# Feed-forward with tokens on the free axis: a feature-major first feed-forward in a two-layer gated cross-attention kernel

## The chip, the cores and the metric

The kernel runs on one core of a Trainium2 chip. A core has a matrix engine (TensorE, PE in the profile; PEld is its loading of the stationary operand), a vector engine (VectorE, DVE), an engine for activation functions (ScalarE, ACT), a general one (GpSimd, POOL) and SyncE (SP), which issues most of the transfers. Each runs its own queue of instructions in order, and semaphores tie the queues together. SBUF is the on-chip memory of 128 partitions; TensorE writes its products to PSUM, 128 partitions in eight banks of 512 fp32 columns. The metric is the device time of one execution in microseconds.

## The reference

Four batches of 512 tokens with 512 features go through two layers, each of a gated cross-attention and a gated feed-forward. The change touches the first layer's feed-forward, and in one place the weights of the second's.

```python
def act_quant(x):                      # per token
    scale = 127.0 / jnp.clip(jnp.max(jnp.abs(x), axis=-1, keepdims=True), EPS)
    q = jnp.clip(jnp.round(x * scale), -128.0, 127.0) / scale
    return q
def weight_quant(w):                   # ternary
    scale = jnp.clip(jnp.mean(jnp.abs(w)), EPS)
    return jnp.clip(jnp.round(w / scale), -1.0, 1.0) * scale
def h_bitlinear(x, w):
    return jnp.einsum('bsh,oh->bso', act_quant(fwht(x)), weight_quant(w))

gate = h_bitlinear(h, w_gate)          # 512 -> 2048
up   = h_bitlinear(h, w_up)            # 512 -> 2048
y    = h_bitlinear(silu(gate) * up, w_down)    # 2048 -> 512
...
x = x + tanh(g_xattn[0]) * L0_xattn(ctx, layernorm(x))   # similarity of 512 x 512, top 153 a row
x = x + tanh(g_ffn[0])   * L0_ffn(layernorm(x))          # the above
x = x + tanh(g_xattn[1]) * L1_xattn(layernorm(x), ctx)   # 16 heads, rotary, softmax
x = x + tanh(g_ffn[1])   * L1_ffn(layernorm(x))          # gated, ternary weights, no Hadamard transform
```

`fwht` is the normalized Walsh-Hadamard transform along the features. The transform of `silu(gate) * up` has length 2048 = 16 x 128. The 8-bit rounding takes a scale from each token's greatest magnitude over all 2048 transformed features.

## The kernel before

**Outer order.** Attention of the second layer (`attention`, L877, class `Pair`) runs over 4 batches times 8 pairs of heads, each in four steps (`scores` L815, `turn` L840, `attended` L848, `added` L861). Everything else is background work written as generators that yield a cost. The loop at L989 advances the attention by one step and then as many parts of the background as the summed costs allow: `before(b)` (L963) for batch b = 1 to 3 during the attention of batch b - 1, that is top-k adjacency (`adjacency`, L410), keys and the first feed-forward (`feed0`, L500); then `last_weights` (L974) and the second feed-forward (`feed1`, L575) of batches 0 to 2 during the attention of batch 3. Batch 0's first feed-forward comes before the attention and batch 3's second feed-forward after it; there the flag `alone[0]` is true, and `feed0` notes it as `quick`. A scheduler of the tile framework orders each engine's queue from the program's order, given priorities and its own cost figures; the top-k instructions get a lowered priority (L446, L451), a few attention products a raised one.

**Buffers.** Background work that is not alone takes its PSUM tiles from two banks (`psb`, tag `bg`): `bg_ps` (L72), `gate_ps` (L75) and `bg_tr` (L78) all come to that. Attention has four banks (`ps`) and two more for its transposes (`pst`). SBUF tiles of 2 KB a partition have pools of two or three (`front_t` L86, `gate_t` L91, `back_t` L96), 8 KB tiles (`big` L101) a pool of three.

**First feed-forward, one tile of 128 tokens.** `zq` holds the quantized, transformed input as [feature, token], four blocks of 128 features in bf16. The weights `wa` are fp8 ternary values, [feature, 2 x 2048], those of `up` first.

- `gated` (L295), four rounds `o` of 512 hidden features: `pg` and `pu`, each [token, 512], from four accumulating products with `zq` as the stationary operand and 512 columns of `wa` moving. ScalarE computes `sg = silu(dg * pg)` straight from PSUM, with `dg` the token's scale per partition (L307), VectorE multiplies by `pu` into `ya` (L308).
- `back` in `feed0` (L545): four butterfly stages on VectorE (eight halves of 1024 columns, L551) make the transform across the 16 blocks of 128. For the transform within blocks, four times: four fp32 transposes (L557), a ScalarE copy (`yT`, L559), four fp32 products of 128 columns with the 128 x 128 Hadamard matrix moving (L563), and a scaled copy to `yb` (L564).
- `projected` (L362): maximum of magnitudes along the 2048 columns (L377), a scale per token (`scales`, L187), multiplication and addition of 12582912, which rounds (L382), subtraction to bf16 (`unmagic`, L205; L210 when not alone), 16 bf16 transposes back to [feature, token] with four ScalarE copies (`turned`, L197), and 16 products of 512 columns with the last weights `wd` (L399). L569 scales and adds to the residual.

`tiles` (L313) weaves the gates of one tile with the back part of the one before it.

**Last weights.** `ternary` (L215) reads each weight matrix in pieces of 1 MB: one pass for the mean magnitude (L234), one for the scaling and addition of 12582912 (L247) and the sign to fp8 (L248), all on ScalarE. With `hold` (first layer) the pieces stay in SBUF between the passes; without (`w1`, twelve pieces) they are read again.

Of the kernel before, what the change touches and what calls it, by code (L numbers as in the profile page):

```python
# [2 lines left out]

# [12 lines left out]
P = 128  # L16
# [10 lines left out]
EPS = 1e-5  # L27
MAGIC = 12582912.0
GONE = -3.0e38
F8 = mybir.dt.float8e4  # L30


@with_exitstack
def flamingo_kernel(
# [43 lines left out]
    def bg_tr(name, dt=F32):  # L78
        if mine("tr", 4):
            return psb.tile([P, 4, P], dt, tag="bg", name=name)  # L80
        return pst.tile([P, 4, P], dt, tag="tr", name=name)
# [14 lines left out]
    def back_t(name):  # L96
        return two_k("back", 2, name)
# [117 lines left out]
    def ternary(specs, names, hold):  # L215


        found = []

        def piece(src, inner, i, name):  # L220
            t = big(f"{name}{i}")
            marks["load"] = nc.sync.dma_start(
                t if inner == 1 else t.rearrange("p (c o) -> p c o", c=inner), src(i)
            )
            return t

        for (src, inner, n, dst, count), name in zip(specs, names):
            acc = small.tile([P, n], F32, tag=f"wacc{n}", name=f"acc_{name}")
            held = []
            for i in range(n):  # L230
                t = piece(src, inner, i, f"sa_{name}")
                held.append(t)
                junk = bp.tile([P, FF], BF, tag="q", name=f"ja_{name}{i}") if hold else t
                nc.scalar.activation(junk, t, AF.Abs, accum_out=acc[:, i : i + 1])  # L234
                yield 4.0
            tot = small.tile([P, 1], F32, tag="wtot", name=f"tot_{name}")
            nc.vector.tensor_reduce(tot, acc, AX.X, ALU.add)
            pt = bg_ps(f"pt_{name}")
            marks["sum"] = nc.tensor.matmul(pt[:, 0:1], ones, tot, start=True, stop=True)
            sc = const.tile([P, 1], F32, tag=f"ws_{name}", name=f"ws_{name}")  # L240
            nc.vector.tensor_scalar(sc, pt[:, 0:1], 1.0 / count, EPS, ALU.mult, ALU.max)
            inv = const.tile([P, 1], F32, tag=f"wi_{name}", name=f"wi_{name}")
            nc.vector.reciprocal(inv, sc)
            found.append(sc)
            for i in range(n):
                t = held[i] if hold else piece(src, inner, i, f"sb_{name}")
                nc.scalar.activation(t, t, AF.Identity, scale=inv, bias=magic[:, 0:1])  # L247
                marks["sign"] = nc.scalar.activation(  # L248
                    dst(i), t, AF.Sign, bias=magic[:, 1:2], saturate=False
                )  # L250
                yield 4.0
        return found
# [42 lines left out]
    def gated(u, zq, wa, dg, y):  # L295

        for o in range(4):
            pg = gate_ps(f"pg_{u}_{o}")
            pu = gate_ps(f"pu_{u}_{o}")
            for pw, at in ((pg, FF + o * 512), (pu, o * 512)):  # L300
                for c in range(NC):
                    nc.tensor.matmul(  # L302
                        pw, zq[:, c, :], wa[:, c, at : at + 512],
                        start=(c == 0), stop=(c == NC - 1),
                    )
            sg = gate_t(f"sg_{u}_{o}")
            nc.scalar.activation(sg, pg, AF.Silu, scale=dg)  # L307
            nc.vector.tensor_tensor(y[:, o * 512 : (o + 1) * 512], sg, pu, ALU.mult)  # L308
            yield 0.9

    reached = []

    def tiles(name, ready, wa, back, spread):  # L313

        def gate(j):
            zq, dg, du = ready[j]
            y = big(f"ya_{name}_{j}")  # L320
            return gated(f"{name}_{j}", zq, wa, dg, y), back(j, y, du)

        def go(gen, parts):
            for _ in range(parts):
                next(gen, None)

        if not alone[0]:
            last = iter(())
            for j in range(NT):
                if j == 2:  # L330
                    reached.append(name)
                front, behind = gate(j)
                yield from woven(front, last)
                last = behind
            yield from last
            return
        if spread:
            lent.extend("btbhtbbt")
        front, cur = gate(0)
        drain(front)  # L340
        last = None
        for j in range(NT):
            front, after = gate(j + 1) if j + 1 < NT else (iter(()), None)
            for k in range(8 if spread else 4):
                if spread:
                    go(cur, 1)
                if k % 2 == 0 or not spread:
                    go(front, 1)
                yield 0.0
            if spread:  # L350
                if last:
                    go(last, 4)
                go(cur, 4)
            else:
                go(cur, 4)
            if last:
                drain(last)
            last, cur = cur, after
        drain(last)
        yield 0.0  # L360

    def projected(u, z, mul, wd, gd, last):  # L362
# [35 lines left out]
        for c in range(NF):  # L398
            nc.tensor.matmul(  # L399
                pd, zT[:, c, :], wd[:, c, :], start=(c == 0), stop=(c == NF - 1)  # L400
            )
        return pd, col


# [95 lines left out]
    def feed0(b, w):  # L500
# [44 lines left out]
        def back(j, ya, du):  # L545
            u = f"f{b}_{j}"
            yb = big(f"yb_{u}")

            for src, dst, g in ((ya, yb, 8), (yb, ya, 4), (ya, yb, 2), (yb, ya, 1)):
                for args in butterfly(src, dst, "p (g t q) -> p g t q", {"g": g}):  # L550
                    nc.vector.tensor_tensor(*args)  # L551
                    yield 1.3
            for k in range(4):
                pt = bg_tr(f"ph_{u}_{k}")
                for c in range(4):
                    at = (4 * k + c) * P
                    nc.tensor.transpose(pt[:, c, :], ya[:, at : at + P], ident)  # L557
                hT_ = back_t(f"yT_{u}_{k}")
                nc.scalar.copy(hT_, pt.rearrange("p c q -> p (c q)"))  # L559
                pz = bg_ps(f"pzh_{u}_{k}")  # L560
                for c in range(4):
                    cols = slice(c * P, (c + 1) * P)
                    nc.tensor.matmul(pz[:, cols], hT_[:, cols], had_sb, start=True, stop=True)  # L563
                nc.scalar.activation(  # L564
                    yb[:, k * 512 : (k + 1) * 512], pz, AF.Copy, scale=1.0 / math.sqrt(FF)
                )
                yield 0.3
            pd, col = yield from projected(u, yb, du, wd, gd, j == NT - 1)
            nc.vector.scalar_tensor_tensor(xs[b, j], pd, col, xs[b, j], ALU.mult, ALU.add)  # L569
            yield 0.8  # L570

# [567 lines left out]
```

## Time and profile before

| | us |
|---|---|
| median of three timed runs | 2063.09 (2061.5 to 2064.79) |
| profiled execution, its own time | 2064.35 |
| its span, first to last instruction | 2062.6 |
| busy: TensorE / weight loads / VectorE | 1853.7 / 873.3 / 1584.7 |
| busy: ScalarE / GpSimd | 1176.6 / 333.1 |
| start of the attention of batches 1, 2, 3 (its transposed input, L722) | 661, 1078, 1495 |
| end of each tile of the first feed-forward (L569), batch 1 | 534, 573, 627, 651 |
| the same, batch 2 | 953, 997, 1038, 1064 |
| the same, batch 3 | 1370, 1414, 1455, 1482 |

How to read it: a row of costly groups names the line, the engine, the operation, the output and inputs by the program's names, shapes and count; then busy time in all, mean ns of one, the engine's idle time just before these instructions, and what ended that. A plain fp32 product appears as two TensorE instructions, a transpose or a bf16/fp8 product as one. Matmuls overlap in the records, so that the mean of one is longer than the spacing between two. Times are from the start of the span.

### The profile page before, as it was taken

What the parts mean: (1) busy time and instruction counts of PE and PEld (TensorE: products, weight loads), DVE (VectorE), ACT (ScalarE), POOL (GpSimd) and SP (SyncE); (2) the same over time, 40 slices, a digit from 0 to 9 for tenths busy, and PEclk for the clock granted to TensorE, in tenths of its full rate; (3) what the DMA queues carried; (4) which work ended last, traced back from release to release, by engine and by line L of the source; (5) the groups of instructions that cost most, each with busy time, mean ns of one, the idle gap of its engine ahead of it and who ended that gap; (6) DMA issues with size and microseconds to landing.
All of it is one profiled execution on the core that took longest, in us unless ns stands there. A gap on an engine that the chain in (4) does not pass through costs nothing. (4 is left out here: it accounts for less than half of the span.)

```text
span 2062.6 us, 21752 instructions
## 1 busy us (share of the span) xinstructions
PE 1853.7 (90%) x7274; PEld 873.3 (42%) x7274; DVE 1584.7 (77%) x3233; ACT 1176.6 (57%) x1979; POOL 333.1 (16%) x316
## 2 busy tenths in 40 slices
PE   1268789999999999999999999999999999999898
PEld 0035434434544444445453444454444444444344
DVE  7989599986774999876769999767636755866775
ACT  6935454455544555455454554554899565567554
POOL 3010031122100221230011221300112210101000
PEclk6579899999999999999999999999999999999999
DMA  7451021210101222110012221101755111111000
GB/s 273 148 177 38 1 77 41 63 46 27 38 21 32 83 82 60 43 38 26 27 33 87 72 73 38 38 21 33 256 191 199 50 38 45 58 35 39 11 16 26
DMA packets 65633, 139.25 MB, mean 68 GB/s; under 512 B 7537, under 2 KB 18161, under 8 KB 62449
## 3 DMA queue, kind: packets, MB, share of 16 engines
q1 hardware_dynamic: 60048, 121.92, 18.7%
q0 software_dynamic: 4320, 14.16, 1.8%
q10 hardware_dynamic: 1152, 1.77, 0.2%
q8 instruction: 58, 0.95, 0.2%
q14 instruction: 55, 0.44, 0.1%
HBM read 117.90 MB, written 19.92 MB: 67 GB/s over the span
## 5 line engine op out<-in xcount | busy, mean ns | idle before, releaser
L793 POOL TENSOR_TENSOR ro<-ro,rs 128x512 f32<-128x512 f32 x192 | 252.7, 1319 | 1167.2 <-DVE rs L789 753.8
L834 ACT ACTIVATE pp<-pss,nm 128x512 f32<-128x512 f32 x256 | 175.1, 688 | 224.8 <-DVE nm L831 224.0
L764 PE MATMUL pqh<-hT,wq 128*128 128x512 f32 x512 | 239.6, 603 | 6.8 <-ACT pp L834 6.6
L853 PE MATMUL pc<-pT,kv 128*128 128x512 f32 x512 | 235.4, 598 | 0.7 <-ACT pT L846 0.6
L865 PE MATMUL po<-om,cxo 128*128 128x512 f32 x512 | 230.9, 597 | 0.0
L831 DVE TENSOR_REDUCE nm<-pss 128x1 f32<-128x512 f32 x256 | 167.6, 681 | 57.4 <-PE pss L826 56.5
L779 PE MATMUL pb<-qh,wc 128*128 128x512 f32 x384 | 191.1, 614 | 10.4 <-ACT qh L769 7.3
L449 DVE MAX8 m<-work 128x8 f32<-128x512 f32 x304 | 198.0, 680 | 0.6
L454 DVE MATCH_REPLACE8 work<-m,work 128x512 f32<-128x512 f32 x288 | 192.8, 674 | 0.1
L837 ACT ACTIVATE pp<-pp,rsm 128x512 f32<-128x512 f32 x256 | 178.9, 724 | 21.2 <-DVE rsm L836 20.9
L870 DVE SCALAR_TENSOR_TENSOR x<-po,gt,x 128x512 f32<-128x512 f32 x128 | 94.6, 744 | 92.4 <-PE po L865 91.9
L846 ACT COPY pT<-ppt 128x512 f32<-128x512 f32 x256 | 142.9, 592 | 28.9 <-PE ppt L845 28.8
L845 PEld LDWEIGHTS ppt<-ident,pp 128*128 128x128 f32 x1024 | 117.3, 141 | 86.0 <-issue 33.9
L845 PE MATMUL ppt<-ident,pp 128*128 128x128 f32 x1024 | 146.4, 277 | 6.7 <-ACT pT L846 3.5
L823 PE MATMUL pss<-kr,qr 64*128 64x512 f32 x256 | 144.3, 644 | 5.6 <-ACT pp L834 4.8
L764 PEld LDWEIGHTS pqh<-hT,wq 128*128 128x128 f32 x512 | 92.7, 191 | 125.4 <-issue 84.6
L826 PE MATMUL pss<-kr,qr 64*128 64x512 f32 x256 | 144.4, 645 | 0.5 <-DVE ro L787 0.5
L865 PEld LDWEIGHTS po<-om,cxo 128*128 128x128 f32 x512 | 93.7, 190 | 114.5 <-issue 98.1
L787 DVE TENSOR_TENSOR ro<-pb,cos_q 128x512 f32<-128x512 f32 x192 | 130.5, 680 | 11.0 <-PE pb L779 10.2
L853 PEld LDWEIGHTS pc<-pT,kv 128*128 128x128 f32 x512 | 92.7, 190 | 102.3 <-issue 88.7
L858 ACT COPY cxo<-pc 128x512 f32<-128x512 f32 x64 | 37.6, 587 | 135.7 <-PE pc L853 135.4
L750 PE MATMUL pr<-ro,wr 128*64 128x512 f32 x192 | 99.8, 613 | 14.3 <-POOL ro L793 12.2
(266 smaller groups left out, 3123.5 us busy)
## 6 DMA issues: line engine op xcount, KB each, us to landing
wq<-in_wqh SPq DMA_DIRECT2D x64, 256.0 KB, 2.7
om<-omd SPq DMA_DIRECT2D x64, 256.0 KB, 2.7
wc<-in_wkcq SPq DMA_DIRECT2D x32, 384.0 KB, 3.1
krd<-krs POOLq DMA_DIRECT2D x32, 256.0 KB, 2.4
kr<-krd SPq DMA_DIRECT2D x32, 256.0 KB, 2.7
sa_w1v<-in_gvT SPq DMA_DIRECT2D x8, 1024.0 KB, 5.3
sb_w1v<-in_gvT SPq DMA_DIRECT2D x8, 1024.0 KB, 5.5
wr<-in_wqr SPq DMA_DIRECT2D x32, 192.0 KB, 2.4
```

What stands on the lines that cost most here:

```text
L449: nc.vector.max(m8[j], cur[j])
L454: nc.vector.match_replace(works[j], m8[j], cur[j], GONE)
L764: nc.tensor.matmul(pq, self.wqs[i][:, c, :], hT[self.b][:, c, :], start=(c == 0), stop=(c == NC - 1),)
L779: nc.tensor.matmul(pb, self.wc[:, at : at + P], self.qhs[i if i < 2 else o], start=True, stop=True)
L793: nc.gpsimd.tensor_tensor(ro, ro, rs, ALU.add)
L826: nc.tensor.matmul(*args, start=True, stop=True)
L831: nc.vector.tensor_reduce(nm, pss[i], AX.X, ALU.max, negate=True)
L834: nc.scalar.activation(pp, pss[i], AF.Exp, bias=nm, accum_out=sm)
L837: nc.scalar.activation(pp, pp, AF.Copy, scale=rs)
L845: nc.tensor.transpose(pt[:, l, :], pp[:, l * P : (l + 1) * P], ident)
L853: nc.tensor.matmul(pc, kv[self.b][:, l, :], self.pT[i][:, l, :], start=(l == 0), stop=(l == NT - 1),)
L865: nc.tensor.matmul(po, self.cxo[i][:, j * P : (j + 1) * P], self.oms[i], start=(i == 0), stop=(i == 1),)
```

## The change

For batches 1 to 3 the first feed-forward stays in [feature, token] from the gates to the last product:

- `gated_turned` takes `wa` as the stationary operand, a block of 128 hidden features at a time, and 128 tokens of `zq` as the moving one: 16 products of 128 columns into each `pg` and `pu`. The token's scale now varies along the free axis, so `dg` is spread into a 128 x 128 tile, transposed by a product with the identity, copied to SBUF as a row, and VectorE multiplies `pg` by it before ScalarE's Silu.
- In `back` the transposes and their copies are left out; the Hadamard matrix is the stationary operand and 512 columns of `ya` move, four products in all.
- `projected_turned` takes the maximum over the 16 blocks (a strided view), transposes the 128 x 128 result, takes the maximum over partitions' values, makes the scale, turns it into a row as above, multiplies all 2048 columns by the row, rounds by an addition and a subtraction in one instruction to bf16, and goes into the last product with no transposes.
- In `ternary` the scaling of pieces that are read again moves from ScalarE to VectorE.

The tile's values in `back` outside these places are as before, and batch 0 keeps the old way (`quick`).

```diff
@@ ternary
-                nc.scalar.activation(t, t, AF.Identity, scale=inv, bias=magic[:, 0:1])
+                if not hold:
+                    nc.vector.tensor_scalar(t, t, inv, MAGIC, ALU.mult, ALU.add)
+                else:
+                    nc.scalar.activation(t, t, AF.Identity, scale=inv, bias=magic[:, 0:1])
@@ new, beside gated
+    def gated_turned(u, zq, wa, dg, y):
+        row = front_t(f"dgr_{u}")
+        nc.vector.tensor_scalar(row[:, :P], ones, dg, None, ALU.mult)
+        pt = bg_ps(f"pdg_{u}")
+        nc.tensor.matmul(pt[:, :P], row[:, :P], ident, start=True, stop=True)
+        nc.scalar.copy(row[:, P : 2 * P], pt[:, :P])
+        row = row[:, P : 2 * P].unsqueeze(1).to_broadcast([P, 4, P])
+        for o in range(4):
+            pg = gate_ps(f"pg_{u}_{o}")
+            pu = gate_ps(f"pu_{u}_{o}")
+            for pw, at in ((pg, FF + o * 512), (pu, o * 512)):
+                for f in range(4):
+                    cols = slice(at + f * P, at + (f + 1) * P)
+                    for c in range(NC):
+                        nc.tensor.matmul(
+                            pw[:, f * P : (f + 1) * P], wa[:, c, cols], zq[:, c, :],
+                            start=(c == 0), stop=(c == NC - 1),
+                        )
+            sg = gate_t(f"sg_{u}_{o}")
+            nc.vector.tensor_tensor(
+                sg.rearrange("p (f t) -> p f t", f=4), pg.rearrange("p (f t) -> p f t", f=4), row, ALU.mult
+            )
+            nc.scalar.activation(sg, sg, AF.Silu)
+            nc.vector.tensor_tensor(y[:, o * 512 : (o + 1) * 512], sg, pu, ALU.mult)
+            yield 0.9
@@ gate(j), in tiles
-            return gated(f"{name}_{j}", zq, wa, dg, y), back(j, y, du)
+            made = gated_turned if spread and not alone[0] else gated
+            return made(f"{name}_{j}", zq, wa, dg, y), back(j, y, du)
@@ new, beside projected
+    def projected_turned(u, z, mul, wd, gd):
+        most = front_t(f"most_{u}")
+        nc.vector.tensor_reduce(
+            most[:, :P], z.rearrange("p (c t) -> p t c", t=P), AX.X, ALU.max, apply_absolute_value=True
+        )
+        yield 2.3
+        pt = bg_tr(f"pmx_{u}")
+        nc.tensor.transpose(pt[:, 0, :], most[:, :P], ident)
+        amax = small.tile([P, 1], F32, tag="amax", name=f"amaxh_{u}")
+        nc.vector.tensor_reduce(amax, pt[:, 0, :], AX.X, ALU.max)
+        m, sc = scales(amax, mul, f"h{u}")
+        nc.vector.tensor_scalar(most[:, P : 2 * P], ones, sc, None, ALU.mult)
+        pt = bg_tr(f"psc_{u}")
+        nc.tensor.matmul(pt[:, 0, :], most[:, P : 2 * P], ident, start=True, stop=True)
+        row = most[:, 2 * P : 3 * P]
+        nc.scalar.copy(row, pt[:, 0, :])
+        col = small.tile([P, 1], F32, tag="cols", name=f"col_{u}")
+        nc.vector.tensor_scalar(col, m, 1.0 / 127.0, gd, ALU.mult, ALU.mult)
+        yield 0.6
+        zv = z.rearrange("p (c t) -> p c t", t=P)
+        nc.vector.tensor_tensor(zv, zv, row.unsqueeze(1).to_broadcast([P, NF, P]), ALU.mult)
+        yield 2.3
+        q = bp.tile([P, NF, P], BF, tag="zT", name=f"zT_{u}")
+        nc.vector.tensor_scalar(q.rearrange("p c t -> p (c t)"), z, MAGIC, MAGIC, ALU.add, ALU.subtract)
+        yield 1.3
+        pd = bg_ps(f"pd_{u}")
+        for c in range(NF):
+            nc.tensor.matmul(pd, q[:, c, :], wd[:, c, :], start=(c == 0), stop=(c == NF - 1))
+        return pd, col
@@ back, in feed0
+                if quick:
                     pt = bg_tr(f"ph_{u}_{k}")
...
                     nc.scalar.copy(hT_, pt.rearrange("p c q -> p (c q)"))
                 pz = bg_ps(f"pzh_{u}_{k}")
+                if quick:
                     for c in range(4):
...
+                else:
+                    cols = slice(4 * k * P, 4 * (k + 1) * P)
+                    nc.tensor.matmul(pz, had_sb, ya[:, cols], start=True, stop=True)
...
-            pd, col = yield from projected(u, yb, du, wd, gd, j == NT - 1)
+            if quick:
+                pd, col = yield from projected(u, yb, du, wd, gd, j == NT - 1)
+            else:
+                pd, col = yield from projected_turned(u, yb, du, wd, gd)
```

More of the change, by code (lines that the diff above doesn't have):

```diff
@@ L1 @@
 import math
-from contextlib import ExitStack
+from contextlib import ExitStack, nullcontext
 import concourse.bass as bass
@@ L29 @@
 GONE = -3.0e38
+U16 = mybir.dt.uint16
 F8 = mybir.dt.float8e4
@@ L401, in projected @@
             )
+        return pd, col
+    def projected_turned(u, z, mul, wd, gd):
+        chunks = "p (c t) -> p c t"
+        most = front_t(f"most_{u}")
[16 more added lines that the diff above has]
+        yield 0.6
+        zv = z.rearrange(chunks, t=P)
+        nc.vector.tensor_tensor(zv, zv, row.unsqueeze(1).to_broadcast([P, NF, P]), ALU.mult)
[6 more added lines that the diff above has]
+            nc.tensor.matmul(pd, q[:, c, :], wd[:, c, :], start=(c == 0), stop=(c == NF - 1))
         return pd, col
@@ L553, in back @@
             for k in range(4):
[L554 to L559, printed above, removed]
-                pz = bg_ps(f"pzh_{u}_{k}")
-                for c in range(4):
-                    cols = slice(c * P, (c + 1) * P)
-                    nc.tensor.matmul(pz[:, cols], hT_[:, cols], had_sb, start=True, stop=True)
+                if quick:
+                    pt = bg_tr(f"ph_{u}_{k}")
+                    for c in range(4):
+                        at = (4 * k + c) * P
+                        nc.tensor.transpose(pt[:, c, :], ya[:, at : at + P], ident)
+                    hT_ = back_t(f"yT_{u}_{k}")
+                    nc.scalar.copy(hT_, pt.rearrange("p c q -> p (c q)"))
+                pz = bg_ps(f"pzh_{u}_{k}")
+                if quick:
+                    for c in range(4):
+                        cols = slice(c * P, (c + 1) * P)
+                        nc.tensor.matmul(pz[:, cols], hT_[:, cols], had_sb, start=True, stop=True)
+                else:
+                    cols = slice(4 * k * P, 4 * (k + 1) * P)
+                    nc.tensor.matmul(pz, had_sb, ya[:, cols], start=True, stop=True)
                 nc.scalar.activation(
```

## The prediction

> **What bounds the kernel now.** I read the engine totals first, then the busy tenths, then windows cut around the stages that the change touches, then the waits inside them. The span is 2062.6 us; the profiled execution took 2064.35 us, 1.75 us around it, and the median of the three timed runs is 2063.09 us, so a difference made in the span carries over to the median one to one.
>
> ```profile
> PE 1853.7 (90%) x7274; PEld 873.3 (42%) x7274; DVE 1584.7 (77%) x3233; ACT 1176.6 (57%) x1979; POOL 333.1 (16%) x316
> ...
> PE   1268789999999999999999999999999999999898
> ...
> DVE  7989599986774999876769999767636755866775
> ACT  6935454455544555455454554554899565567554
> ```
>
> TensorE is full from about 250 us on. VectorE is full only in the three stretches of top-k work (a row of nines in each batch), ScalarE only around slices 29 to 31. The windows say it by stage; the columns are busy time (instructions) of TensorE, its weight loads, VectorE, ScalarE, GpSimd, then granted clock, DMA share, GB/s.
>
> ```profile
> 665.00:870.00 205.00, 196.85 (x625) 85.19 (x624) 196.44 (x438) 104.23 (x204) 42.46 (x38) 1.00 0.22 68
> 905.00:1066.00 161.00, 157.10 (x721) 80.26 (x719) 111.07 (x160) 83.53 (x152) 19.94 (x14) 1.00 0.09 25
> 1320.00:1482.00 162.00, 157.22 (x729) 80.29 (x728) 111.16 (x158) 94.45 (x164) 20.70 (x14) 1.00 0.23 75
> 1490.00:1585.00 95.00, 86.54 (x270) 38.13 (x269) 43.84 (x90) 90.98 (x111) 15.29 (x12) 0.96 0.65 221
> ```
>
> The first is the top-k of batch 2, the second and third are the first feed-forward's gates, Hadamard and last product for batches 2 and 3, the fourth is the scaling of the last weights. In the feed-forward stages TensorE is busy 97.6% and 97.0%, VectorE 69%, ScalarE 52% and 58%. So there a TensorE microsecond removed is worth close to a microsecond, and VectorE has some 50 us free in each. In the fourth ScalarE is busy 96% and TensorE falls to 91%.
>
> **TensorE, per tile of batches 1 to 3 (12 tiles).** Busy means of matmuls overlap, so I take start-to-start times from the order of time (start, length, line, tiles, count):
>
> ```profile
> 566.61 0.61 PE L202 MATMUL ptq_hf<-identb,q_f 128*128 128x128 bf16 x8
> 567.05 1.08 PE L853 MATMUL pc<-pT,kv 128*128 128x512 f32 x2
> 567.97 0.61 PE L202 MATMUL ptq_hf<-identb,q_f 128*128 128x128 bf16 x8
> ...
> 573.65 1.02 PE L853 MATMUL pc<-pT,kv 128*128 128x512 f32 x2
> 574.50 1.03 PE L302 MATMUL pu_f<-wa_w,zq_f 128*128 128x512 fp8e4 x4
> ...
> 576.23 1.03 PE L302 MATMUL pg_f<-wa_w,zq_f 128*128 128x512 fp8e4 x4
> 577.09 1.03 PE L302 MATMUL pu_f<-wa_w,zq_f 128*128 128x512 fp8e4 x4
> ...
> 1047.01 1.16 PE L563 MATMUL pzh_f<-had_sb,yT_f 128*128 128x128 f32 x8
> 1048.01 0.60 PE L557 MATMUL ph_f<-ident,ya_f 128*128 128x128 f32 x4
> 1048.45 0.82 PE L845 MATMUL ppt<-ident,pp 128*128 128x128 f32 x6
> ```
>
> Removed: 32 gate products of 512 columns, four in 0.86 us: 6.88. 16 fp32 transposes, four in 0.44: 1.76. The Hadamard products of 128 columns: a plain fp32 product is recorded as two instructions, eight take 1.00, four such groups: 4.00. 16 bf16 transposes of the quantized tile, eight in 0.44: 0.88. Together 13.52 us.
>
> Added: four fp32 Hadamard products of 512 columns, 0.85 each (the pair at 573.65): 3.40. Two 128-column fp32 products and one transpose for the scale row, the gate row and the maxima: five records of about 0.11: 0.55. And 128 gate products of 128 columns, each with a weight load of its own. No fp8 tile is a stationary operand in this trace; the nearest row is the bf16 transpose, which also loads a new stationary tile for every 128 columns. Its longest run:
>
> ```profile
> 2019.96 0.83 PE L202 MATMUL ptq_hg<-identb,q_g 128*128 128x128 bf16 x12
> 2020.63 0.38 PE L302 MATMUL pg_g<-wa_w,zq_g 128*128 128x512 fp8e4 x1
> ```
>
> Twelve in 0.67 us, 56 ns each, so 128 take 7.17. Added: 11.12 us; net -2.40 a tile, **-28.8 us** for twelve.
>
> Here the Trainium skill speaks against the change: "TensorE: Matmul & The Clock Gate", section "Back-to-back issue gap", puts a sustained stream of load-and-multiply pairs at about 81 ns for 128 columns, well above the gap of an isolated product. By that, an estimate, the gates take 10.37 us, not 7.17: 3.2 more a tile, 38.4 in all, and the sum turns to +9.6. I take 56 because it is measured here with loads in it and over twelve pairs; but a gate round is 32 pairs, and no run of 32 is shown, so 81 stays as the upper end. Below 56 I have no row; the lower end is 56.
>
> **Handovers.** After a run of bf16 transposes the next pair of fp32 products takes 0.92 us (567.05 to 567.97), after gate products 0.85: the weight load no longer hides behind a short product, 0.07 a change. Eight changes come in a tile and two go: 6 x 0.07 x 12 = **+5** (0 to 9).
>
> **TensorE's waits.** Gone with the copies between transpose and Hadamard product are L563's idle 3.9 us over 16 tiles, for twelve **-3**. New is a longer chain in the gates: product, multiplication by the row on VectorE, Silu on ScalarE, product with `up` on VectorE, in the same two PSUM buffers. Behind the waiting `pu` of the next round stand the attention's products in TensorE's order, and for those wait ScalarE's exponentials. Now the waits are small, because attention's products fill the rounds (573.65 and 575.37 above):
>
> ```profile
> L302 PE MATMUL pg_f<-wa_w,zq_f 128*128 128x512 fp8e4 x256 | 66.9, 382 | 0.6 <-ACT zq_f L203 0.5
> L302 PE MATMUL pu_f<-wa_w,zq_f 128*128 128x512 fp8e4 x256 | 66.5, 379 | 1.1 <-ACT sg_f L307 0.8
> L302 PE MATMUL pg_g<-wa_w,zq_g 128*128 128x512 fp8e4 x256 | 67.0, 383 | 5.3 <-ACT sg_g L307 5.3
> L302 PE MATMUL pu_g<-wa_w,zq_g 128*128 128x512 fp8e4 x256 | 66.7, 382 | 4.1 <-DVE ya_g L308 2.9 <-DVE res_g L640 0.7 <-ACT sg_g L307 0.2
> ```
>
> The added step is one VectorE operation of 0.68 (L308) and some queueing, some 1.4 us a round; over 48 rounds the ends are 0, all covered, and 67, none. I take what the second feed-forward's gates wait, 9.4 us over 16 tiles, for twelve **+7**.
>
> **VectorE, per tile.** Added: four multiplications of 512 by the row (0.68: 2.73), a 2048-wide tensor product (2 x 1.23 by L551, less one start-up, about 2.3), two 128-wide scalings (0.2 each) and a 128-wide maximum (about 0.3): 5.7. Removed: the 2048-wide scale of L382, 1.28. The 2048-wide maximum (2.28) now reads with a stride; no row shows that, I take the same, at the worst twice. Conversion stays (1.38 before; then an add and a subtract in one). Net +4.4, or 17.8 in a batch, lifting VectorE in a feed-forward stage from 69% to 80%. What that costs TensorE is bounded by the top-k window: VectorE at 96%, TensorE still at 96.0% against 97.6%. 1.6% of three stages of 165 us is 8 us; I take **+3**. If the cover were gone, 53 us of VectorE work would stand on the path.
>
> **ScalarE.** Eight copies of 0.59 go, two of 128 columns (about 0.27) come: -4.2 a tile. ScalarE has 40% free in these stages; nothing is taken for it.
>
> **Last weights.** Twelve 2048-wide scalings of 2.10 us (25 us) leave ScalarE and become 12 x 1.28 = 15.4 on VectorE, 46% busy there. Were TensorE as busy as elsewhere (97%) in that window of 95 us, 6 us would come back. But VectorE now stands at the queue's head for each 1 MB load (5.5 us to landing), with attention's maxima (`nm`) queued behind it and the exponentials waiting for these. From -6 to +6, I take **-4**. No DMA is added or moved; the loads keep their place on SP.
>
> **Sum.** -28.8 + 5 - 3 + 7 + 3 - 4 = -20.8 us: 2063.1 - 20.8 = **2042 us**, 1.0% faster. Its own range is 2025 to 2056.
>
> **Rivals.**
> 1. *Pairs are slower in long runs* (nearer to 81 ns). For: 256 instructions a tile come where 64 came, and TensorE's waits named "issue" exist. Against: 56 ns over twelve. Break-even is 20.8 us / 1536 products = 13.5 ns more, 69.5 ns; at 81 it is 2042 + 38 = 2080, at 75 ns 2071.
> 2. *Slower than before through the gate rounds*: the three-step chain in two PSUM buffers is not filled by attention, and TensorE stands 1.4 us a round before `pu`. For: VectorE's queue holds 1.2 and 2.3 us operations of the Hadamard stages just then. Against: 1.7 us of such waits in the rows now. It decides from (20.8 + 7) / 1.4 = 20 of 48 rounds; with 25 uncovered, 2070.
> 3. *The saved products leave idle time*: attention's own chain (scores, maximum, exponential, turn) sets the pace, and TensorE only falls to a lower share. For: TensorE's waits on attention's ScalarE copies. Against: 97% busy. Then only some 5 of 28.8 us arrive after the costs: 2058, or no difference at all.
>
> **How the numbers follow.** The forecast's case 0.60, the first rival 0.12, the second 0.13, the third 0.15. A measurement tells about 0.2% (4 us) from no change: below 2059 is faster, above 2067 slower. Faster: 0.60 of the first, 0.10 of the third, 0.01 of the others: 0.71. Same: 0.05 and 0.02: 0.07. Slower: 0.22. For eight times in ten I go from 2022 (chains covered, handovers free, the weights' 6 us) to 2076 (between the first rival at 75 and at 81 ns).
>
> **What would show it.** Right: gate products spaced 56 to 60 ns; TensorE's busy sum about 25 us lower; yT and the turned bf16 tiles gone for batches 1 to 3; `pu_f` idle under 10 us; ScalarE under 85% with the last weights. Wrong: a spacing over 70 ns; tens of us of idle before `pu_f` or `pzh_f` put down to VectorE; TensorE's share falling with the span unchanged; a strided maximum near 4.5 us.

## The result and the profile after

The changed kernel takes 2088.74 us in the median of five runs (2078.19 to 2089.75), the kernel before 2063.09 us beside it: a ratio of 1.0104 with a 95% interval of 1.009 to 1.0119. The change makes the kernel about 1% slower; the forecast was 1% faster, and the time lies above its whole range. The profiled execution took 2086.08 us with a span of 2084.3 us, so the two profiles show the difference in full. The medians are 25.6 us apart and the means 22.0, because one of the five runs of each kernel lies 7 to 12 us from the others. From here on, microseconds against the kernel before are the ratio less one times 2064: +21.5 us for the change (18.6 to 24.6).

Where did it arise? The first transpose of the attention's input (`phT`, on TensorE) of each batch marks a batch's start; the table of the profile before has its copies on ScalarE, 1 to 2 us later. Before they stand at 260, 659, 1076 and 1494 us, after at 259, 662, 1088 and 1514. The last start to the end of the span is 568.7 us before and 570.3 after. The loss lies in the three stretches with the first feed-forward, which are 4, 9 and 8 us longer, and the stretch with the last weights gives nothing back. These are differences of one execution of each kernel, as everything that is read from traces below.

Engine totals and busy tenths of the changed kernel:

```profile
PE 1844.9 (89%) x7814; PEld 874.2 (42%) x7814; DVE 1668.5 (80%) x3329; ACT 1107.8 (53%) x1893; POOL 336.8 (16%) x316
...
PE   1278799999899999998899999989889999999898
...
DVE  7989599987876999878779999787858555866775
ACT  6935543454434554454344554534686565567554
```

VectorE gained 84 us and ScalarE lost 69. TensorE, nines throughout these stretches before, shows eights where the feed-forwards of batches 1 to 3 stand. The windows of the changed kernel (columns as in the prediction; the granted clock follows the five busy sums):

```profile
895.00:1089.00 194.00, 178.21 (x1004) 92.98 (x1002) 153.04 (x236) 82.90 (x156) 26.61 (x21) 0.97 0.11 30
1320.00:1515.00 195.00, 175.71 (x999) 91.80 (x998) 152.80 (x236) 97.27 (x169) 26.84 (x21) 0.98 0.24 78
1515.00:1610.00 95.00, 88.17 (x267) 38.38 (x266) 66.64 (x135) 71.59 (x106) 17.23 (x12) 0.95 0.67 226
969.00:978.00 9.00, 6.31 (x8) 2.64 (x9) 6.80 (x11) 5.49 (x10) 2.54 (x2) 0.62 0.00 1
```

In the feed-forward stages of batches 2 and 3 TensorE is busy 92% and 90%, where it was 97.6% and 97.0%, and the granted clock is 0.97 and 0.98, where it was 1.00. VectorE stands at 79% and 78%, ScalarE with the last weights at 75%. The groups of the changed kernel that carry the new work:

```profile
L634 PE MATMUL pzh_f<-ya_f,had_sb 128*128 128x512 f32 x96 | 52.7, 684 | 10.2 <-DVE ya_f L617 9.8
L331 PE MATMUL pu_f<-zq_f,wa_w 128*128 128x128 bf16 x768 | 50.7, 219 | 2.5 <-DVE ya_f L340 2.3
L442 DVE TENSOR_REDUCE most_f<-yb_f 128x128 f32<-128x2048 f32 x12 | 43.9, 3662 | 14.5 <-ACT yb_f L635 14.5
L336 DVE TENSOR_TENSOR sg_f<-pg_f,dgr_f 128x512 f32<-128x512 f32 x48 | 33.1, 690 | 16.5 <-PE pg_f L331 15.9
L249 DVE TENSOR_SCALAR sb_w1v<-sb_w1v,wi_w1v 128x2048 f32<-128x2048 f32 x8 | 11.0, 1372 | 6.5 <-DMA sb_w1v<-in_gvT 6.4
L447 PE MATMUL pmx_f<-ident,most_f 128*128 128x128 f32 x12 | 3.8, 319 | 10.5 <-DVE most_f L442 10.5
```

TensorE waits 9.8 us for the butterflies (`pzh_f`) and 10.5 us for the strided maximum (`pmx_f`), which takes 3.66 us. Before `pu_f`, where the prediction had placed its worst case, it waits 2.5 us only.

The order of time shows how. First VectorE of the kernel before in the stretch of batch 2 where the last gate rounds of one tile (L308) stand among the butterflies (L551), and TensorE's first instruction that needs them:

```profile
961.70 0.68 DVE L308 TENSOR_TENSOR ya_f<-sg_f,pu_f 128x512 f32<-128x512 f32 x1
962.30 2.36 DVE L551 TENSOR_TENSOR yb_f<-ya_f 128x1024 f32<-128x1024 f32 x2
964.57 0.69 DVE L308 TENSOR_TENSOR ya_f<-sg_f,pu_f 128x512 f32<-128x512 f32 x1
965.17 2.36 DVE L551 TENSOR_TENSOR ya_f<-yb_f 128x1024 f32<-128x1024 f32 x2
966.91 0.66 PE L557 MATMUL ph_f<-ident,ya_f 128*128 128x128 f32 x4
967.44 0.69 DVE L789 TENSOR_TENSOR rs<-pb,sin_q 128x512 f32<-128x512 f32 x1
```

VectorE has no gap here. Its share over the whole stage is 69%, but from the first gate round at 955.96 to the last butterfly at 967.53 it does nothing but this chain. TensorE does not wait for it, though: products of the gates and of the attention fill its queue until its first transposes begin at 966.91, while the last butterfly is still running, and over all tiles it waits 0.1 us there:

```profile
L557 PE MATMUL ph_f<-ident,ya_f 128*128 128x128 f32 x256 | 40.7, 289 | 0.1
```

So the chain ended just in time. Now the same place in the changed kernel, with two gate groups of TensorE ahead and the maximum behind:

```profile
955.73 1.06 PE L331 MATMUL pg_f<-zq_f,wa_w 128*128 128x128 bf16 x16
956.62 1.06 PE L331 MATMUL pu_f<-zq_f,wa_w 128*128 128x128 bf16 x16
...
962.79 0.69 DVE L336 TENSOR_TENSOR sg_f<-pg_f,dgr_f 128x512 f32<-128x512 f32 x1
963.39 1.22 DVE L617 TENSOR_TENSOR ya_f<-yb_f 128x1024 f32<-128x1024 f32 x1
964.52 0.68 DVE L340 TENSOR_TENSOR ya_f<-sg_f,pu_f 128x512 f32<-128x512 f32 x1
965.12 1.23 DVE L617 TENSOR_TENSOR ya_f<-yb_f 128x1024 f32<-128x1024 f32 x1
966.26 0.69 DVE L336 TENSOR_TENSOR sg_f<-pg_f,dgr_f 128x512 f32<-128x512 f32 x1
...
969.72 0.69 DVE L905 TENSOR_REDUCE nm<-pss 128x1 f32<-128x512 f32 x1
970.32 2.36 DVE L617 TENSOR_TENSOR ya_f<-yb_f 128x1024 f32<-128x1024 f32 x2
971.69 6.75 PE L634 MATMUL pzh_f<-ya_f,had_sb 128*128 128x512 f32 x8 [4.13 <-DVE ya_f L617]
...
979.11 3.64 DVE L442 TENSOR_REDUCE most_f<-yb_f 128x128 f32<-128x2048 f32 x1 [3.31 <-ACT yb_f L635]
```

The row multiplications (L336) stand in the queue between the butterflies. From the first of them at 956.89 to the last butterfly at 972.68 it takes 15.8 us where it took 11.6: four row multiplications at a spacing of 0.60 us, a maximum of the attention (`nm`, 0.6) and an idle stretch of 1.1. TensorE has used up the products that stand ahead of `pzh_f` in its queue by 967.56 and stands 4.13 us. Then the clock is granted at half speed: the eight records take 6.75 us, at 0.43 us each they would be 3.4. One late chain thus costs some 7 us; the last line of windows above is this place (TensorE 6.31 of 9 us, clock 0.62).

For a ledger I took TensorE's start-to-start times from the first batch's start to the fourth's. Each record gets its undisturbed spacing in these traces (0.429 us for 512 fp32 columns, 0.2155 for 512 fp8 columns, about 0.11 for 128 fp32, 0.056 for 128 bf16), the sum of which is the work. What exceeds it while the clock is halved is the clock's loss, and any other excess over 60 ns is a wait. A remainder of -67 to -70 us (records that start sooner than their spacing) is not shown. The ledger is this document's own sum and no view prints it; only its differences are read, because the wait column also holds excesses in which TensorE was not idle. The profile's busy time of TensorE in the same stretch, the first batch's start to the fourth's (before, then after), checks it:

```profile
260.40:1493.90 1233.50, 1182.66 (x4520) 555.26 (x4518) 1013.83 (x2026) 641.64 (x1207) 237.12 (x216) 1.00 0.18 57
259.10:1514.00 1254.90, 1169.80 (x5059) 554.65 (x5057) 1083.21 (x2108) 596.91 (x1132) 238.90 (x216) 0.99 0.18 54
```

| kernel | stretch | work | halved clock | waits |
|---|---|---|---|---|
| before | 1233.5 | 1110.1 | 3.7 | 187.9 |
| after | 1254.9 | 1086.6 | 10.3 | 225.0 |
| flat_max | 1242.9 | 1086.6 | 8.9 | 214.9 |
| no_gate_row | 1234.6 | 1083.9 | 4.3 | 216.5 |
| no_row_flat_max | 1221.0 | 1083.9 | 2.5 | 205.0 |
| before_extra_op | 1238.5 | 1110.1 | 2.4 | 191.8 |
| before_gate_chain | 1249.5 | 1110.1 | 10.8 | 194.5 |
| pu_drained | 1248.8 | 1086.6 | 11.0 | 218.1 |
| folded_max_drained | 1229.7 | 1086.6 | 5.0 | 204.7 |
| late_max | 1292.5 | 1086.6 | 20.2 | 250.0 |

TensorE's work fell by 23.5 us. The waits rose by 37.1 us and the halved clock's loss by 6.6, which is 20 us more than the change saved. By the windows TensorE's idle time rose from 50.8 to 85.1 us, by 34.3, close to the ledger's 37.1.

### The profile page after: what moved, and what is told of

Read it like the earlier page. It is cut to its first block, busy times and chain, and to the rows that moved or that the text cites. A ratio compares the mean times of both kernels' runs of the same rounds, so it can differ in the third digit from the quotient of the medians.

```text
span 2084.3 us, 22859 instructions
## 1 busy us (share of the span) xinstructions
PE 1844.9 (89%) x7814; PEld 874.2 (42%) x7814; DVE 1668.5 (80%) x3329; ACT 1107.8 (53%) x1893; POOL 336.8 (16%) x316
## 5 line engine op out<-in xcount | busy, mean ns | idle before, releaser
L919 PEld LDWEIGHTS ppt<-ident,pp 128*128 128x128 f32 x1024 | 117.3, 142 | 85.1 <-issue 37.9
```

The lines of the kernel that those rows point to most:

```text
L919: nc.tensor.transpose(pt[:, l, :], pp[:, l * P : (l + 1) * P], ident)
```

## The experiments

Two accounts were on trial. By the first (V where a letter stands for it) VectorE's added work is what costs. By the second (L) it is the length of the chain of engines between a product and the release of its PSUM bank: whatever adds a station to it costs, on VectorE or not. Beside them stood the strided maximum and the last weights.

One caution holds for all of them. The framework's scheduler orders the queues anew for each kernel. In flat_max TensorE's instructions stand in the same order as in the changed kernel, and in no_row_flat_max as in no_gate_row; there the edit alone is measured. In the other runs of the feed-forward's parts attention's and background's products also stand in a different order, so that a difference is the edit's together with the new order's, and no run here takes the two apart.

**weights_only**: the kernel before with the last weights scaled on VectorE, nothing else.

```diff
-nc.scalar.activation(t, t, AF.Identity, scale=inv, bias=magic[:, 0:1])
+if not hold:
+    nc.vector.tensor_scalar(t, t, inv, MAGIC, ALU.mult, ALU.add)
+else:
+    nc.scalar.activation(t, t, AF.Identity, scale=inv, bias=magic[:, 0:1])
```

> The kernel before with one part of the change alone: the twelve scalings of the last weights on VectorE. Theory V (the feed-forward's added VectorE work stands in its own chain, TensorE waits in order behind it and its clock halves): this part is worth little, -4 to +4 us on 2063. Theory W (VectorE at the head of its queue waits for the weights' transfers and holds attention up): most of the 25 us lost are here, 2078 or more.

Measured: ratio 1.0013 (1.0003 to 1.0023), +3 us (0.6 to 4.7). The part brings nothing.

**feed_forward_only**: the changed kernel with that edit taken back.

> The changed kernel with the weights' scaling back on ScalarE, so the feed-forward's part alone. Theory V: 2083 to 2091, as the changed kernel. Theory W: at or under 2068.

Measured: 1.011 (1.0094 to 1.0126), as slow as the whole change. The loss is the feed-forward's.

**flat_max**: each maximum over as many columns, but neighbouring ones, which are not the tokens' maxima.

```diff
-most[:, :P], z.rearrange("p (c t) -> p t c", t=P), AX.X, ALU.max, ...
+most[:, :P], z.rearrange("p (t c) -> p t c", t=P), AX.X, ALU.max, ...
```

> The changed kernel with the 2048-wide maximum taken over neighbouring columns instead of columns 128 apart (the same number of elements in and out, but the maxima are not the tokens', so the output isn't the reference's). It takes away the stride alone: the changed trace has 3.64 us for the strided one, 2.28 is expected. Theory S (the strided maximum, in whose shadow TensorE waits, is the loss): 12 x 1.36 = 16 us back and two or three half-clock windows gone, 2065 to 2071. Theory V with the gates' multiplications as the greater part: 5 to 10 us back, 2077 to 2082.

Measured: 1.0054 (1.0037 to 1.0071), so 10 us of the 21.5 come back. The groups:

```profile
L634 PE MATMUL pzh_f<-ya_f,had_sb 128*128 128x512 f32 x96 | 51.1, 668 | 10.1 <-DVE ya_f L617 9.8
...
L442 DVE TENSOR_REDUCE most_f<-yb_f 128x128 f32<-128x2048 f32 x12 | 27.4, 2283 | 14.6 <-ACT yb_f L635 14.6
...
L447 PE MATMUL pmx_f<-ident,most_f 128*128 128x128 f32 x12 | 3.5, 291 | 1.1 <-DVE most_f L442 1.1
```

The stride alone makes 2.28 us into 3.66. TensorE's wait at `pmx_f` falls from 10.5 to 1.1 us, the wait at `pzh_f` stays. The maximum's price is that wait, nearly one for one (9.4 us of wait, 10 us of time).

**no_gate_row**: no row and no multiplication by it; Silu reads PSUM with a scale per partition again, which is the wrong scale here.

```diff
-nc.vector.tensor_tensor(sg..., pg..., row, ALU.mult)
-nc.scalar.activation(sg, sg, AF.Silu)
+nc.scalar.activation(sg, pg, AF.Silu, scale=dg)
```

> The changed kernel without the gates' row: ScalarE takes Silu straight from PSUM with a scale per partition as before (which is the wrong scale here, so the output isn't the reference's), and neither the row is made nor VectorE multiplies by it. It takes 12 x (4 x 0.69 + 0.2) = 36 us from VectorE and one step from the gates' chain. Theory V: 20 us or more back, 2058 to 2067. Theory S: only a few, 2082 to 2086.

Measured: 1.0005 (0.9994 to 1.0017): 20 us come back, the largest part of the loss. The groups:

```profile
L625 PE MATMUL pzh_f<-ya_f,had_sb 128*128 128x512 f32 x96 | 48.0, 629 | 1.6 <-DVE ya_f L608 1.5
L438 PE MATMUL pmx_f<-ident,most_f 128*128 128x128 f32 x12 | 3.8, 318 | 13.3 <-DVE most_f L433 13.3
```

The wait at `pzh_f` goes from 9.8 to 1.5 us, the one at `pmx_f` grows by 2.8. In the ledger the waits fall by 8.5 us, the halved clock's loss by 6.0 and the work by 2.7, the products that make the row.

**no_row_flat_max**: both edits.

> The changed kernel without the gates' row (Silu with the wrong, per-partition scale) and with the maximum over neighbouring columns (not the tokens' maxima): both of the larger VectorE additions gone, TensorE's new products all there; the output isn't the reference's. Theory V (TensorE's saving is real and VectorE's additions eat it): the two recoveries, 22 us and 10 us, add up: 2050 to 2058, below the kernel before. Theory O (what is lost is the order and the shape of TensorE's new work, not VectorE): no lower than no_gate_row, 2063 to 2068.

Measured: 0.9943 (0.9926 to 0.9959), 12 us faster than before. The two add up: 10 and 20 us singly, 33 together. With both gone, about half of TensorE's saving appears in the time. What remains of the new waits is 205.0 + 2.5 - 187.9 - 3.7 = 16 us in the ledger.

**before_extra_op** and **before_gate_chain**: the kernel before with one more VectorE operation of 512 columns in each of the 48 rounds. In the first it stands behind Silu, ahead of the product with `pu`; in the second it stands ahead of Silu, between TensorE and ScalarE, as in the changed kernel.

```diff
 nc.scalar.activation(sg, pg, AF.Silu, scale=dg)
+nc.vector.tensor_tensor(sg, sg, sg, ALU.max)
```

```diff
-nc.scalar.activation(sg, pg, AF.Silu, scale=dg)
+nc.vector.tensor_scalar(sg, pg, dg, None, ALU.mult)
+nc.scalar.activation(sg, sg, AF.Silu)
```

> The kernel before with one more VectorE operation of 512 columns in each gate round of batches 1 to 3 (the greater of sg and sg, so no value changes), nothing taken from TensorE: 48 x 0.68 = 33 us of VectorE. Theory V: +12 to +30 us on 2064, that is 2076 to 2094. If VectorE's 31% of idle time in these stages covered it, as the prediction had it, 2064 to 2068.

> The kernel before with the changed gates' chain and nothing else of the change: in batches 1 to 3 VectorE scales pg from PSUM (by the token's scale per partition, 0.7 us), then Silu reads SBUF, then VectorE multiplies by pu; the result is the same. VectorE's load is that of before_extra_op (33 us, +7 us there, where the operation stood behind Silu); only its place differs, between TensorE and ScalarE. If VectorE's time alone counts: 2069 to 2073. If the place counts (TensorE to VectorE to ScalarE to VectorE): 2078 to 2088.

Measured: 1.0036 (1.0027 to 1.0045) for the first, 1.0069 (1.0051 to 1.0087) for the second: +7 and +14 us. The groups of the first, then of the second:

```profile
L309 DVE TENSOR_TENSOR sg_f<-sg_f 128x512 f32<-128x512 f32 x48 | 34.8, 724 | 14.6 <-ACT sg_f L307 14.6
```

```profile
L308 DVE TENSOR_SCALAR sg_f<-pg_f,dg_f 128x512 f32<-128x512 f32 x48 | 35.9, 747 | 14.2 <-PE pg_f L302 13.3
L309 ACT ACTIVATE sg_f<-sg_f 128x512 f32<-128x512 f32 x48 | 30.3, 631 | 60.6 <-DVE sg_f L308 60.5
```

VectorE's load is the same within 2 us, the price is twice as high: 7 us (5.6 to 9.3) and 14 us (10.5 to 18.0). So 33 us of added load cost about 7, and the other place some 7 more. That these are a price for each round is not shown. The profiled execution of before_gate_chain took 2084.14 us, 6 us above its median, and 8 us of its difference to before_extra_op lie in the first of the three stretches (408.3 us against 400.3). There the next instruction in TensorE's queue is a transpose of the last tile of batch 1, for which it stands 4.72 us, and within this wait the clock is halved for 6.8 us:

```profile
656.02 1.03 PE L202 MATMUL ptq_hf<-identb,q_f 128*128 128x128 bf16 x8 [4.72 <-DVE q_f L210]
```

Whether the longer chain or the new order of the queues brought the tile there so late is open.

**gate_row_gpsimd**: the multiplication goes to GpSimd, with ScalarE copying the product to SBUF ahead of it. VectorE is freed of 48 operations that took 33 us, and the chain gets longer.

```diff
-nc.vector.tensor_tensor(sg..., pg..., row, ALU.mult)
+nc.scalar.copy(sg, pg)
+nc.gpsimd.tensor_tensor(sg..., sg..., row, ALU.mult)
```

> The changed kernel with the gates' multiplication by the row moved off VectorE: ScalarE copies pg from PSUM, GpSimd (busy 16%) multiplies in SBUF, Silu and the rest as they are; the result is the same. The gates' chain becomes longer (0.6 + 1.3 us instead of 0.69), VectorE's load smaller by 33 us. Theory V (it is VectorE's time): 2060 to 2070. Theory L (it is the length of the gates' chain in two PSUM buffers): 2087 to 2100.

Measured: 1.0157 (1.0142 to 1.0172), 11 us slower than the change itself. The groups:

```profile
L338 POOL TENSOR_TENSOR sg_f<-sg_f,dgr_f 128x512 f32<-128x512 f32 x48 | 63.8, 1329 | 133.2 <-ACT sg_f L336 133.0
L617 DVE TENSOR_TENSOR yb_f<-ya_f 128x1024 f32<-128x1024 f32 x64 | 93.9, 1490 | 6.9 <-PE pzh_f L634 6.0 <-PE ph_f L624 0.9
...
L331 PE MATMUL pu_f<-zq_f,wa_w 128*128 128x128 bf16 x768 | 50.7, 219 | 15.6 <-DVE ya_f L340 14.7 <-ACT sg_f L336 0.9
```

GpSimd takes 1.33 us for what VectorE does in 0.69. Now TensorE does stand before `pu_f`, 15.6 us, for the bank that the last product of the chain frees. But the run does not take VectorE's time away as it was meant to. The butterflies, for which TensorE waits, became longer. In the changed kernel they are

```profile
L617 DVE TENSOR_TENSOR yb_f<-ya_f 128x1024 f32<-128x1024 f32 x64 | 80.3, 1268 | 6.0 <-PE pzh_f L634 6.0
```

and here 1.49 us on average: of the 128 in both directions, the 45 that run at the same time as one of GpSimd's operations take 1.75 us, the other 83 take 1.22. VectorE's busy time falls by 11 us only, from 1668.5 to 1657.4, and the wait at `pzh_f` stays, at 10.4 us. So the run shows that the GpSimd form is worse, and not which account is right.

**gpsimd_row_folded_max**: the same, and the strided maximum replaced. ScalarE writes magnitudes of each 512 columns (`AF.Abs`), VectorE folds them by maxima of whole pieces and then of their halves, 512 columns down to 128.

```diff
+nc.scalar.activation(size, pz, AF.Abs, scale=1.0 / math.sqrt(FF))
+nc.vector.tensor_tensor(most, most, size, ALU.max)
 ...
-nc.vector.tensor_reduce(most[:, :P], z.rearrange("p (c t) -> p t c", t=P), ...)
+nc.vector.tensor_tensor(most[:, :256], most[:, :256], most[:, 256:], ALU.max)
+nc.vector.tensor_tensor(most[:, :P], most[:, :P], most[:, P : 2 * P], ALU.max)
```

> gate_row_gpsimd, and the strided maximum replaced: ScalarE also writes the magnitudes of each 512 columns, VectorE folds them by maxima of neighbours as they come (3 x 0.68 + 0.4 + 0.3 = 2.7 us instead of 3.64, of which only 1.4 us lie behind the last piece); the result is the same. Theory V: 10 us below gate_row_gpsimd, 2048 to 2060, which would beat the kernel before. Theory L: 2080 or more.

Measured: 1.0109 (1.0092 to 1.0126), 10 us below the run before it. The folded form recovers what flat_max did, and the GpSimd form keeps its price.

**late_max**: the transpose of the maxima gets a lower priority, so that other products stand ahead of it in TensorE's queue.

```diff
+with tc.high_priority(offset=-FILL // 4):
     nc.tensor.transpose(pt[:, 0, :], most[:, :P], ident)
```

> The changed kernel with one instruction of each tile moved: the transpose of the maxima (pmx), for which TensorE stands 12.5 us in the changed trace, gets a lower priority in the written order, so that attention's products that are ready go ahead of it; nothing else changes and the result is the same. Theory P (TensorE stands there because its order was written for a 2.3 us maximum and the strided one takes 3.64): the waits at pmx go, 2075 to 2080, as flat_max. Theory V (VectorE's time itself): the wait moves on to the next product that needs the tile, 2084 to 2091.

Measured: 1.0283 (1.0263 to 1.0303), 37 us worse than the change. Neither account had this. The groups:

```profile
L468 PE MATMUL pd_f<-wd_w,zT_f 128*128 128x512 fp8e4 x192 | 50.4, 423 | 19.5 <-DVE zT_f L464 19.5
...
L796 PE MATMUL phT<-ident,nq 128*128 128x128 f32 x64 | 10.2, 311 | 8.7 <-DVE nq L184 8.0 <-ACT hT L797 0.7
...
L448 PE MATMUL pmx_f<-ident,most_f 128*128 128x128 f32 x12 | 3.7, 310 | 7.3 <-DVE most_f L442 7.3
```

The expectation's 12.5 us are 10.5 in the row of the changed kernel. The wait at `pmx_f` falls by 3 us only and moves on to the end of the same chain, `pd_f`, with 19.5 us, and to the next batch's first input. The batch starts drift to 680, 1117 and 1555 us. A batch's feed-forward must be done before its attention can begin, so a later chain has nowhere to hide. The clock stood at half speed for 72 us between 250 and 1600 us, against 37.5 in the changed kernel and 17 before.

**pu_drained**: the chain is left, but ScalarE copies `pu` out of PSUM, and the last product runs in SBUF.

```diff
-nc.vector.tensor_tensor(y[:, o * 512 : (o + 1) * 512], sg, pu, ALU.mult)
+nc.scalar.copy(yo, pu)
+nc.vector.tensor_tensor(yo, yo, sg, ALU.mult)
```

> The changed kernel with pu copied out of PSUM by ScalarE (48 x 0.6 us, which ScalarE has free), so that its bank is free before VectorE's multiplication; VectorE's work is the same in count, the result too. Theory L (the longer gates' chain holds the two PSUM banks): 2065 to 2078. Theory V: 2084 to 2095.

Measured: 1.0058 (1.0043 to 1.0073): 9.5 us come back with 48 operations more on ScalarE and none fewer on VectorE. VectorE's work alone as the cause falls here. The groups:

```profile
L636 PE MATMUL pzh_f<-ya_f,had_sb 128*128 128x512 f32 x96 | 52.4, 678 | 10.6 <-DVE ya_f L619 10.6
L331 PE MATMUL pu_f<-zq_f,wa_w 128*128 128x128 bf16 x768 | 50.8, 219 | 0.3
L449 PE MATMUL pmx_f<-ident,most_f 128*128 128x128 f32 x12 | 3.8, 319 | 10.4 <-DVE most_f L444 10.4
```

The wait for the bank (`pu_f`) falls from 2.5 to 0.3 us, the two large waits stay. That the held bank is a part of the price fits, but it is seen for some 2 us; where the rest comes from is not shown.

**folded_max_drained**: the changed kernel with pu_drained's edit and the folded maximum.

> The changed kernel with pu drained by ScalarE and the maximum folded from magnitudes that ScalarE writes; the gates' row stays on VectorE and the result is the same. If the two recoveries add (10 us each of 25): 2063 to 2070, no better than before. If the strided maximum's wait only moves: 2075 or more.

Measured: 0.9976 (0.9965 to 0.9988), 5 us faster than before, which is better than either expectation: 26.5 us come back, where the two parts gave 9.5 and some 10. The groups:

```profile
L331 PE MATMUL pu_f<-zq_f,wa_w 128*128 128x128 bf16 x768 | 50.7, 219 | 0.3
...
L634 PE MATMUL pzh_f<-ya_f,had_sb 128*128 128x512 f32 x96 | 47.9, 619 | 4.6 <-ACT pp L915 2.9 <-DVE ya_f L617 1.7
...
L447 PE MATMUL pmx_f<-ident,most_f 128*128 128x128 f32 x12 | 3.6, 300 | 2.3 <-DVE most_f L444 2.3
```

The waits at `pzh_f` for VectorE (9.8 to 1.7), `pmx_f` (10.5 to 2.3) and `pu_f` (2.5 to 0.3) are nearly gone together, with the row multiplication kept. Neither part alone moved the one at `pzh_f` (10.6 us in pu_drained, 9.8 in flat_max), so the two are not independent.

**drained_act_weights**: that, with the last weights' scaling back on ScalarE.

> folded_max_drained with the last weights' scaling back on ScalarE; the result is the same. The two runs on that part gave +1.5 us (weights_only against before) and -2.6 us (feed_forward_only against the changed kernel). If ScalarE's added copies and magnitudes lie before the weights' stage: 2056 to 2062. If it needs VectorE's help there by now: 2063 to 2068.

Measured: 0.9968 (0.9956 to 0.998); the median is 2056.07 us against 2063.72 us of the kernel before. It is the fastest version that computes what the change computes, and beats both kernels. It isn't told apart from folded_max_drained: the intervals overlap.

**scaled_input_folded_max** and **half_scaled_folded_max**: the gate's scale is multiplied into the quantized input when it is made bf16, which rounds it once more than the reference does, so that the result is not quite the reference's; in the second every bf16 tile of the kernel is fp16. There is no row and no multiplication in the rounds, and the maximum is the folded one.

```diff
-unmagic(q, h)
+nc.vector.tensor_scalar(q, h, MAGIC, dg, ALU.subtract, ALU.mult)
+du = ratio
 ...
-nc.vector.tensor_tensor(sg..., pg..., row, ALU.mult)
-nc.scalar.activation(sg, sg, AF.Silu)
+nc.scalar.activation(sg, pg, AF.Silu)
```

> The changed kernel with both VectorE additions answered in another way: the token's scale is multiplied into the quantized input in the instruction that already converts it to bf16 (so gates and up need no row, at bf16 rounding of the scaled input), Silu reads PSUM directly, and the maximum is folded from magnitudes that ScalarE writes. Theory V: as no_row_flat_max, 2048 to 2058, which beats the kernel before. If the remaining additions (the 2048-wide multiplication by a row, the turned scale) decide, 2063 or more.

> scaled_input_folded_max with fp16 in place of bf16 for the quantized tiles (whole numbers up to 127 are exact in both; the scaled input now keeps 11 bits). Same instructions and sizes: 2046 to 2054, below the kernel before. If fp16 products are slower than bf16 here, more than 2060.

Measured: 0.9923 (0.9907 to 0.994) and 0.9934 (0.9919 to 0.9949). They show what the change could bring without its two new costs: 14 to 16 us.

## Why the prediction was wrong

*TensorE's work: right in the main.* The sum had -28.8 + 5 = -23.8 us; the ledger has -23.5. That they agree to 0.3 us is partly luck: the ledger's work has no handovers in it, and it counts the removed Hadamard products at 0.11 us each, where the prediction took 0.125 (5.8 us in all). The gate groups start 0.89 us apart over 16 products (955.73 to 956.62), 56 ns each, with fp8 tiles as stationary operands. The Trainium skill's page "TensorE: Matmul & The Clock Gate", section "Back-to-back issue gap", gives about 81 ns, the first rival's ground; the trace does not agree. In 28 places a `pg` and a `pu` follow each other without a break, the 32 pairs of which the prediction had no run, and they too start every 56 ns. The first rival's 2080 us is the nearest number in the prediction, by a mechanism that did not occur. The busy sum fell by 8.8 us only, not 25: records overlap, and they lengthen while the clock is halved. It was the wrong thing to name as a sign.

*TensorE's waits (+7, with -3 for the copies gone) and VectorE (+3): here it failed.* These steps allowed +7 us together; the ledger has 37.1 + 6.6 = 43.7. The 6.6 are the halved clock, for which the sum had no term. The step's load was about right: VectorE came to 79% of the stage where 80% was forecast, and gained 84 us in all where 53 + 15 were forecast; the stride is the rest. Its error was to price the load by the stage's mean, with "some 50 us free", and by the top-k window, where over half of VectorE's work (106.7 of 196.4 us) is the top-k itself, placed at a lowered priority, and not a chain like this one. The free time is not where the operations land. In the stretch from 955.96 to 967.53 of the kernel before VectorE has no gap, and it ends as TensorE comes to need it; 4.2 us more there became a wait of 4.13 us. The trace shown above had this ahead of the change; only a window of 161 us was read.

*The gates as the place of the wait.* The second rival had the mechanism (a longer chain in two banks, with butterflies in VectorE's queue) and the sign, at 2070 us. But it looked for the wait before `pu_f`, at 1.4 us a round. It came to 2.5 us there and 9.8 at `pzh_f`, later in TensorE's queue and named in the prediction only as a sign of being wrong, and was worsened by the clock. Removing the row gives 20 us back. The pair of runs on the kernel before puts some 7 us on the load and some 7 on the place ahead of Silu, and pu_drained gets 9.5 us back with the row kept. These overlap, the order of the queues changes with each, and an exact split is open.

*The strided maximum.* "The same, at the worst twice" bounded it well, at 3.66 us against 2.28. But the sum took nothing for the stride, and the worst case was thought of as VectorE's load only. The transpose of the maxima stands in TensorE's queue behind it, so the stride cost 10 us as a direct wait: flat_max removes it and the time with it, with every instruction of TensorE in the same place.

*Last weights (-4): nothing.* ScalarE fell from 96% to 75% in that stage, as said, yet weights_only is at +3 us (0.6 to 4.7), and taking the edit back gains nothing that can be told. Of the two effects weighed against each other the second shows in the groups: VectorE stands 6.4 us for loads (L249) with the attention's work queued behind it. That this is the cause was only argued.

*The third rival*, that saved products leave idle time, falls by half: with row and stride gone, 12 us of 23.5 arrive, with the folded maximum and scaled input 16, more than its 5. But TensorE's idle time is 67.8 us in the stretch of no_row_flat_max, against 50.8 before.

What stays open: some 16 us of the new waits are there without row and stride, spread over many places. The wider multiplication by the second row (2.30 us, before 1.28) and the round trips for the maxima and the scale row are candidates, and none was run alone. That stalls bring the halved clock is read from the order of time and wasn't tried by itself. In the changed kernel each half-speed window between 551 and 1524 us begins during a wait of 1.6 to 4.1 us or within 3 us of its end; a wait of 2.5 us at 570 us was followed by none.

## What to carry to other kernels

Price an operation added to a shared engine in the stretch where it will stand, instruction by instruction: an engine at 69% of a stage can be without a gap in the 12 us that release the bottleneck. An added station between a product and the release of its PSUM bank can cost by its place as well as its load (here 14 us against 7 for the same 48 operations, with the order of the queues changed too), and copying the other operand out of PSUM is worth a try (9.5 us here). When an operation is moved to another engine to test a cause, check that the instructions left behind keep their length. Where a reduction's result is waited for, count its longer duration as a wait of the engine behind it and not as load, and reduce along neighbouring columns.

## What the hardware showed unexpectedly

- A reduction of 128 x 2048 fp32 magnitudes to 128 x 128 takes 2.28 us along neighbouring columns and 3.66 us with a step of 128 columns (512 bytes), the same instruction otherwise.
- A wait of 4.13 us of TensorE in an otherwise full stretch was followed by several microseconds at half clock, which cost another 3.3 us. Such half-speed stretches sum to 17 us between 250 and 1600 us before and 37.5 after, to 72 in late_max.
- fp8 tiles of 128 columns as stationary operands with 128 bf16 columns moving start every 56 ns in groups of 16 and 32, as bf16 transposes do in groups of 12.
- VectorE's additions and subtractions of 128 x 1024 fp32 in SBUF take 1.22 us alone and 1.75 us on average where they overlap GpSimd's operations on 128 x 512 fp32 in SBUF (83 and 45 of them in gate_row_gpsimd).
